# Half sets of exponentials on VectorE in a fused attention and graph-layer kernel

## Chip, cores and metric

The kernel runs on one core of a Trainium2 chip. The metric is the device time in microseconds (us) from the launch's first to its last instruction; runs of the same kernel agree within about 0.03% here. All matrix work is in fp32 or in the fp32r form, nothing is in bf16.

## What is computed

The reference takes 3327 tokens `x` of width 128 and a weighted adjacency matrix `adj` (3327 x 3327), and applies four layers, each followed by a residual and a layer norm. Cut to what matters here:

```python
# layer 0: attention with 128 heads of width 8, adj added twice to the scores
q = (x @ Wq.T).reshape(d, n, h)          # d = 128 heads, h = 8
k = (x @ Wk.T).reshape(d, n, h)
v = (x @ Wv.T).reshape(d, n, h)
a = jnp.einsum('dnh,dmh->dnm', q, k) * d ** -0.5 + adj + adj
a = jax.nn.softmax(a, axis=2)
out = jnp.einsum('dnm,dmh->dnh', a, v).reshape(n, h * d) @ Wo.T
# layer 1: a_norm @ (x @ W.T + b), a_norm from adj + I and its row sums
# layer 2: (adj / rowsum) @ x @ W_in + (adj.T / colsum) @ x @ W_out
# layer 3: x @ W_self.T + (adj @ x) @ W_neigh.T + b
# after every layer: x = layernorm(x + layer)
```

There are 128 x 3327 x 3327 = 1.4 billion exponentials in layer 0. They are the work that the change is about. The column sums of `adj` are used in layer 2 alone.

## The kernel before

**Stages.** A first stage (about 0 to 297 us) projects `x` to queries, keys and values and stores them. `attention()` (297 to 9970 us) is layer 0. A last stage (from 9970 us) divides by the softmax sums, multiplies by `Wo`, and does layers 1 to 3 as dense products with `adj`, 26 row tiles each (`gather`, L1110). A function `wide_attention`, taken when scores could overflow, does not run with these inputs.

**Blocks, heads, sets.** `attention()` goes over 7 query chunks of 476 columns (CW) and, inside each, 4 key blocks of 7, 7, 6 and 6 key tiles of 128 keys (KBS): 28 blocks, called kind 0, 1, 2 and 3 here by their place in the chunk. In a block it goes over 128 heads `d`. The key tiles of a head are taken in three *sets*: 3, 2 and 2 tiles for a block of 7, 2, 2 and 2 for a block of 6 (SETS). Each of the three sets has its own score buffer in PSUM, `sc0`, `sc1`, `sc2`, one bank of 512 columns for each tile. Four heads make a *group* (12 sets, numbered p0 to p11 below), of which there are 32 in a block.

**One set** (`exponents`, L616). TensorE adds two or three score products to the buffer (L632; the buffer holds the edge weights and earlier heads' scores, so that each head takes the previous scores out as it adds its own). Then the exponentials are read out of PSUM into an SBUF tile `e`: by ScalarE in one activation of 952 or 1428 columns (L640), or, for some sets, by VectorE (`vector_exp`, L590): a clamp and scale to an integer that reads PSUM (L596), two bit operations on it in SBUF (L597, L599), and a polynomial of degree five as five `scalar_tensor_tensor` in SBUF (L602), one after the other. Only L596 holds the score buffer. TensorE cannot add the next head's scores to a buffer until it has been read. A set goes whole to VectorE where `on_vector` (L454) says so for the group and it is p2 of its group: 24 of 32 groups in kind 0, all 32 in kind 1, 28 in kinds 2 and 3.

**Weighing** (`weigh`, L647). The sums over keys of a group are taken while the next group's exponentials are made: for each key tile, four products `values x e` for the four heads side by side (L658), into one bank `o`, 8 instructions (each fp32 product goes in two). After which sets of the next group they are placed on TensorE's queue is written in PLACES (blocks of 6: after p0, p2, p4, p6, p8, p10; blocks of 7: p1, p1, p4, p6, p8, p10, p10), FULL (kind 0, a pattern for each of four groups in turn) and FIRST (the first group of a block). Every third group `flush` copies or adds `o` into `acc` on VectorE (L669, L671) before `o` can be used again.

**Order.** TensorE's, ScalarE's, VectorE's and GpSimd's queues run in the order in which the program emits instructions (`manual_schedule`, L685 and after). VectorE's polynomial steps wait in a list `vec` and are emitted by `vector_work` (L607) before each set, as long as a model clock of VectorE (`clock[1]`, a cost in us for each step) is behind a model clock of ScalarE (`clock[0]`, 0.95 or 0.84 a set). VectorE also turns query rows for the next group in kind 0 (`copy_queries`, L517 to L519) and, in the background, transposes `adj` and takes its maxima, row sums and column sums by pieces (`piece_work`, L213: L218, L223, L225, L229 to L233), 91 pieces, one in eight groups.

Of the kernel before, what the change touches and what calls it, by code (L numbers as in the profile page):

```python
# [19 lines left out]
P = 128  # L20
# [10 lines left out]
POLY = (-0.12145248055458069, 1.287218689918518, 0.8447736501693726, 0.7106341123580933, 0.24892811477184296)  # L31
# [19 lines left out]
def kernel(ctx: ExitStack, tc: tile.TileContext, x, adj, wq, wk, wv, wo,  # L51
# [83 lines left out]
    colsum = const.tile([P, T], F32, name="colsum")  # L135
# [20 lines left out]
    csum = const.tile([P, NP // 32], F32, name="csum")  # L156
# [56 lines left out]
    def piece_work(pool, u, c, ai):  # L213

        nj = PIECE // 32
        w = min(PIECE, N - c * PIECE)
        at = pool.tile([P, nj, 4, 32], F32, name="at")
        nc.vector.transpose(at.rearrange("p j t b -> p t j b"), ai.rearrange("p t (j a) -> p t j a", a=32))  # L218
        yield at
        if c == 0:  # L220
            maxima[u] = pool.tile([P, 4, NPC], F32, name="pmax")
            sums[u] = pool.tile([P, 4, NPC], F32, name="psum")
        nc.vector.tensor_reduce(maxima[u][:, :, c], ai[:, :, 0:w], AX.X, ALU.max)  # L223
        yield at
        nc.vector.tensor_reduce(sums[u][:, :, c], ai[:, :, 0:w], AX.X, ALU.add)  # L225
        yield at
        part = csum[:, c * nj:(c + 1) * nj]
        if u == 1:
            nc.vector.tensor_reduce(part, at.rearrange("p j t b -> p j (t b)"), AX.X, ALU.add)  # L229
        else:  # L230
            cs = pool.tile([P, nj], F32, name="cs")
            nc.vector.tensor_reduce(cs, at.rearrange("p j t b -> p j (t b)"), AX.X, ALU.add)
            nc.vector.tensor_tensor(part, part, cs, ALU.add)  # L233
        yield at

    def store_tops(pool, u, top, n):

        hi = pool.tile([P, 4], F32R, name="rhi")
        nc.vector.tensor_copy(hi, top)
        lo = pool.tile([P, 4], F32R, name="rlo")  # L240
        nc.vector.tensor_tensor(lo, top, hi.bitcast(F32), ALU.subtract)
        for row, sb in enumerate((hi, lo)):
            for i in range(P // n):
                nc.gpsimd.dma_start(out=flat_ap(lead_s[u], row * SUPER + i * P, [[1, n], [n, 4]]),
                                    in_=sb[n * i:n * i + n, :].bitcast(F32))
# [172 lines left out]
    def attention():  # L418
        with tc.tile_pool(name="ed", bufs=1) as ed, tc.tile_pool(name="kq", bufs=3) as kq, \
# [11 lines left out]
            o = psc.tile([P, 512], F32, name="o")  # L431
            subs = [(j, min(P, CW - j)) for j in range(0, CW, P)]
# [21 lines left out]
            def on_vector(kb, g):  # L454

                return g % 4 != 0 if kb == 0 else KBS[kb][1] == 7 or g % 8 != 0
# [5 lines left out]
            PLACES = {7: (1, 1, 4, 6, 8, 10, 10), 6: (0, 2, 4, 6, 8, 10)}  # L462
# [79 lines left out]
            loaded, worked, turning = [], [], []  # L542

            def background(n):
                if n % PACE == 2 and worked:
                    piece_store(pe, *worked.pop(0))
# [4 lines left out]
            def background_work(n):  # L551
                if n % PACE == 4 and loaded:
                    u, c, ai = loaded.pop(0)
                    steps = piece_work(pe, u, c, ai)
                    worked.append((u, c, next(steps)))
                    next(steps)
                    clock[1] += 2.4
                    turning.append(steps)
                if n % PACE == 0 and turning:
                    clock[1] += 2.4  # L560
                    for _ in turning.pop():
                        pass

            def prepare(b, d):

                n = b * NHG + d // GROUP
                if d % GROUP == 0:
                    while any(of is None for _, of, _ in vec):
                        vec.pop(0)[2]()
# [12 lines left out]
                if n + 1 < len(groups) and blocks[groups[n + 1][0]][1] == 0 \  # L582
                        and d % GROUP == 1 - on_vector(blocks[b][1], d // GROUP):
# [6 lines left out]
            def vector_exp(e, x, of):  # L590


                y = ex.tile([P, 2, CW], F32, name="ey")
                t = ex.tile([P, 2, CW], F32, name="et")
                yi, ti = y.bitcast(I32), t.bitcast(I32)
                nc.vector.tensor_scalar(yi, x, -58 * math.log(2.0), 2 ** 24 / math.log(2.0), ALU.max, ALU.mult)  # L596
                vec.append((0.7, of, lambda: nc.vector.tensor_scalar(ti, yi, UPPER, EXPONENT, ALU.bitwise_and,  # L597
                                                                 ALU.bitwise_xor)))
                vec.append((0.7, of, lambda: nc.vector.tensor_scalar(yi, yi, LOWER, QUARTER, ALU.bitwise_and,  # L599
                                                                 ALU.bitwise_or)))  # L600
                for i, a in enumerate(POLY):
                    vec.append((1.2, of, lambda i=i, a=a: nc.vector.scalar_tensor_tensor(  # L602
                        e, e if i else y, a, t if i == len(POLY) - 1 else y, ALU.add, ALU.mult)))

            clock = [0.0, 0.0]

            def vector_work(b):  # L607

                while vec and clock[1] < clock[0]:
                    cost, _, step = vec.pop(0)  # L610
                    step()
                    clock[1] += cost
                clock[0] += 0.95 if KBS[blocks[b][1]][1] == 7 else 0.84
                clock[1] = max(clock[1], clock[0] - 1)

            def exponents(b, d, si):  # L616
# [19 lines left out]
                if on_vector(kb, d // GROUP) and (d % GROUP, si) == (0, 2):  # L636
                    vector_exp(e[:, 0:n, :], s[:, 0:n, 0:CW], (b, d // GROUP))
                    clock[1] += 1.2
                else:
                    nc.scalar.activation(e[:, 0:n, :], s[:, 0:n, 0:CW], AF.Exp, scale=2.0)  # L640
# [6 lines left out]
            def weigh(b, g, r):  # L647
# [6 lines left out]
                while any(of == (b, g) for _, of, _ in vec) and r >= SETS[len(queue_of)][2][0]:  # L654
                    vec.pop(0)[2]()
                for j in range(GROUP):
                    c = 32 + (tl * GROUP + j) * 32 - u * A1
                    nc.tensor.matmul(o[32 * j:32 * j + 32, 0:CW], lhsT=values[b, g][:m, c:c + 32],  # L658
# [6 lines left out]
            def flush(b, f):  # L665
                kb = blocks[b][1]
                clock[1] += 0.7
# [7 lines left out]
            def store(b, f):  # L675
                nb = min(PACK, NHG - f * PACK)
                for j in range(GROUP):
                    nc.gpsimd.dma_start(  # L678
# [6 lines left out]
            with tc.manual_schedule(engines={mybir.EngineType.PE, mybir.EngineType.Activation,  # L685
# [8 lines left out]
                for b, d in steps:  # L694
# [3 lines left out]
                    for si in range(len(SETS[KBS[blocks[b][1]][1]])):  # L698
                        vector_work(b)
# [335 lines left out]
    pick = act.tile([P, 32], F32, name="pick")  # L1035
    nc.vector.tensor_tensor(pick, ident[:, 0:32], ident[:, 32:64], ALU.add)
    nc.vector.tensor_tensor(pick, pick, ident[:, 64:96], ALU.add)
    nc.vector.tensor_tensor(pick, pick, ident[:, 96:128], ALU.add)
    ps = bank(7)
    nc.tensor.matmul(ps[0:32, 0:NP // 32], lhsT=pick, rhs=csum, start=True, stop=True)  # L1040
    for q in range(4):
        nc.vector.tensor_copy(colsum[32 * q:32 * q + 32, :],
                              ps[0:32, 0:NP // 32].rearrange("a (s q) -> a q s", q=4)[:, q, :])

# [17 lines left out]
    inv_col = inverse_degree(colsum, "inv_col")  # L1062
# [34 lines left out]

    def gather(t, y, col, b, meanwhile=()):
# [13 lines left out]
        for _, what in todo:  # L1112
            what()
        return ps
# [4 lines left out]
    def divide(t):  # L1119
# [7 lines left out]
        nc.gpsimd.tensor_tensor(ons[t][:n], o[:n, 0:H, :], rec[:n, :].unsqueeze(1).to_broadcast([n, H, D]), ALU.mult)  # L1127
# [38 lines left out]
    with tc.manual_schedule(engines={mybir.EngineType.PE, mybir.EngineType.SP}):  # L1166
# [18 lines left out]
        for t in range(T):  # L1185
# [9 lines left out]
            norm(n, h[:n, :], xs[1][:n, t, :])  # L1195

# [77 lines left out]
```

## Times and profile before

| what | us |
|---|---|
| median of 3 runs (10736.26 to 10739.44) | 10736.91 |
| profiled execution | 10739.45 |
| its span, first to last instruction | 10737.5 |
| granted TensorE clock over the span | 0.996 |
| one block of kind 0, of kind 1, of kind 2 or 3 | about 368, 368, 320 |
| from the last exponential to the end | about 771 |

The blocks' lengths are read off the timeline, from the first edge transposition of a block (L625) to that of the next. The profile's page gives busy time and share of the span for each engine, a picture of the span in 40 slices, the chain that ended last, and the costliest groups of instructions, each with its count, busy time, mean duration, and the idle time of its engine just before it with what ended that idle time. Durations of neighbouring instructions of one engine overlap a little: ScalarE's activations of 952 columns last about 1.0 us each in the profile, but follow each other every 0.844 us in the timeline. [...]

### The profile page before, as it was taken

How to read it: one execution, taken by the hardware profiler on the slowest of the kernel's cores; microseconds unless marked ns; L12 is line 12 of the kernel's file. 1: busy time of each engine (PE TensorE's matmuls, PEld its weight loads, DVE VectorE, ACT ScalarE, POOL GpSimd, SP SyncE). 2: the span in 40 equal slices, each digit the busy share in tenths (PEclk: the TensorE clock that was granted, in tenths of full speed). 3: DMA queues.
4: the chain of work that ended last, by engine and by line, in shares of the span. 5: the costliest groups of instructions: out<-in, count | busy, mean ns of one | idle time of the engine just before them, and what ended most of it. 6: DMA issues, size and time to landing. Idle time of an engine off the chain costs nothing. (4 is left out here: it accounts for less than half of the span.)

```text
span 10737.5 us, 200822 instructions
## 1 busy us (share of the span) xinstructions
PE 10565.1 (98%) x76941; PEld 4105.8 (38%) x76941; DVE 7960.2 (74%) x8554; ACT 9584.8 (89%) x10447; POOL 1554.7 (14%) x2739
## 2 busy tenths in 40 slices
PE   8899999999999999999999999999999999999999
PEld 5333333333333333333333333333333333333779
DVE  6777888777888777887788777888777777777412
ACT  3899999999999999999999999999999999999400
POOL 0111121111221111211122110121111100001200
PEclk9999999999999999999999999999999999999999
DMA  7678886788876888768887588886888867788676
GB/s 270 181 184 188 209 210 181 181 192 201 213 188 171 198 201 209 190 166 200 198 211 196 156 191 191 199 199 172 193 195 202 193 162 179 181 189 196 219 283 246
DMA packets 1013760, 2116.43 MB, mean 197 GB/s; under 512 B 206759, under 2 KB 730985, under 8 KB 998979
## 3 DMA queue, kind: packets, MB, share of 16 engines
q1 hardware_dynamic: 932014, 1985.55, 74.4%
q0 software_dynamic: 79392, 116.16, 3.5%
q8 instruction: 623, 10.21, 0.4%
q14 instruction: 335, 2.74, 0.1%
q10 hardware_dynamic: 1396, 1.77, 0.1%
HBM read 1863.03 MB, written 239.54 MB: 196 GB/s over the span
## 5 line engine op out<-in xcount | busy, mean ns | idle before, releaser
L640 ACT ACTIVATE e<-sc 128x952 f32<-128x952 f32 (+1 forms) x9968 | 9360.0, 1085 | 312.1 <-PE sc L632 284.3
L658 PE MATMUL o<-e,v_pad 128*32 128x476 f32 (+1 forms) x46592 | 5647.1, 573 | 39.4 <-DVE acc L671 18.5
L632 PE MATMUL sc<-qt,kt 64*128 64x476 f32 x23296 | 4491.6, 440 | 52.9 <-ACT e L640 33.5
L632 PEld LDWEIGHTS sc<-qt,kt 64*128 64x128 f32 x23296 | 2184.3, 184 | 4433.6 <-ACT e L640 3740.6
L602 DVE SCALAR_TENSOR_TENSOR e<-e,ey 128x952 f32<-128x952 f32 x2352 | 2707.0, 1151 | 77.4
L596 DVE TENSOR_SCALAR ey<-sc 128x952 int32<-128x952 f32 x784 | 901.1, 1149 | 1411.5 <-PE sc L632 1389.9
L658 PEld LDWEIGHTS o<-e,v_pad 128*32 128x32 f32 (+1 forms) x46592 | 1035.2, 108 | 1907.4 <-issue 1885.1
L533 POOL COPY v_pad<-vs 128x192 f32<-128x192 f32 (+1 forms) x896 | 444.5, 522 | 8018.6 <-DMA vs<-v_img 6214.0
L602 DVE SCALAR_TENSOR_TENSOR e<-ey 128x952 f32<-128x952 f32 x784 | 903.4, 1152 | 27.2
L602 DVE SCALAR_TENSOR_TENSOR e<-e,et 128x952 f32<-128x952 f32 x784 | 901.2, 1149 | 22.3
L253 POOL DMA_DIRECT2D adjT_s<-at x1352 | 760.1, 570 | 132.7 <-DMA adjT_s<-at 92.6
L599 DVE TENSOR_SCALAR ey<-ey 128x952 int32<-128x952 int32 x784 | 519.7, 663 | 27.1
L597 DVE TENSOR_SCALAR et<-ey 128x952 int32<-128x952 int32 x784 | 518.3, 661 | 26.9
L1110 PE MATMUL bank<-y,eT 128*128 128x128 f32 (+1 forms) x4056 | 473.9, 276 | 0.4 <-DVE h L1232 0.4
L1110 PEld LDWEIGHTS bank<-y,eT 128*128 128x128 f32 (+1 forms) x4056 | 465.3, 192 | 5.7 <-DVE h L1232 0.6
L671 DVE TENSOR_TENSOR acc<-o,acc 128x476 f32<-128x476 f32 x231 | 150.3, 651 | 281.5 <-PE o L658 280.9
L517 DVE TENSOR_SCALAR qt<-qt 32x1428 fp32r<-32x1428 f32 x224 | 201.7, 900 | 103.2 <-DMA qt<-q_s 89.2
L519 DVE CAST qt<-qt 64x1904 fp32r<-64x1904 f32 x224 | 260.4, 1163 | 7.6
L1070 ACT ACTIVATE rstd<-mv,eps 128x1 f32<-128x1 f32 x104 | 30.4, 292 | 263.6 <-DVE mv L1068 263.6
L678 POOL DMA_DIRECT2D o_s<-acc x308 | 199.4, 651 | 35.4 <-DVE acc L671 20.8
L1213 PE MATMUL bank<-a,y 128*128 128x512 f32 (+2 forms) x364 | 145.5, 562 | 0.0
L362 ACT ACTIVATE hi<-pp 128x1024 fp32r<-128x1024 f32 x52 | 53.0, 1024 | 87.9 <-PE pp L308 86.3
(148 smaller groups left out, 2274.7 us busy)
## 6 DMA issues: line engine op xcount, KB each, us to landing
qt<-qimg SPq DMA_DIRECT2D x1344, 476.0 KB
kt<-k_s SPq DMA_DIRECT2D x5316, 96.0 KB
kt<-k_s SPq DMA_DIRECT2D x1762, 128.0 KB
eT<-adjT_s SPq DMA_DIRECT2D x78, 1664.0 KB
qimg<-qt SPq DMA_DIRECT2D x224, 476.0 KB
vs<-v_img SPq DMA_DIRECT2D x224, 224.0 KB
adjT_s<-at POOLq DMA_DIRECT2D x1352, 32.0 KB, 4.8
vs<-v_img SPq DMA_DIRECT2D x224, 192.0 KB
```

What stands on the lines that cost most here:

```text
L253: nc.gpsimd.dma_start(out=flat_ap(adjT_s, (t * P + 32 * q) * NP + c * PIECE, [[NP, 32], [P, ns], [1, P]]), in_=at[32 * i:32 * i + 32].rear ...
L517: return [(0.9, None, lambda: nc.vector.tensor_scalar(qt[32:64, 1:], qf[0:32, 0:GROUP - 1], -1.0, None, ALU.mult)), (0.4, None, lambda: nc ...
L519: (1.2, None, lambda: nc.vector.tensor_copy(qt[64:128], qf[0:64]))]
L533: nc.gpsimd.tensor_copy(vp[:, 32:32 + nt * GROUP * 32].rearrange("p (x c) -> p x c", c=32)[:, :, 0:H], vs.rearrange("p (x c) -> p x c", c=H))
L596: nc.vector.tensor_scalar(yi, x, -58 * math.log(2.0), 2 ** 24 / math.log(2.0), ALU.max, ALU.mult)
L597: vec.append((0.7, of, lambda: nc.vector.tensor_scalar(ti, yi, UPPER, EXPONENT, ALU.bitwise_and, ALU.bitwise_xor)))
L599: vec.append((0.7, of, lambda: nc.vector.tensor_scalar(yi, yi, LOWER, QUARTER, ALU.bitwise_and, ALU.bitwise_or)))
L602: vec.append((1.2, of, lambda i=i, a=a: nc.vector.scalar_tensor_tensor(e, e if i else y, a, t if i == len(POLY) - 1 else y, ALU.add, ALU.m ...
L632: nc.tensor.matmul(s[:, i, 0:CW], lhsT=kt[64 * rg:64 * rg + 64, k, pos * P:(pos + 1) * P], rhs=qt[64 * rg:64 * rg + 64, k, :], start=False ...
L640: nc.scalar.activation(e[:, 0:n, :], s[:, 0:n, 0:CW], AF.Exp, scale=2.0)
L658: nc.tensor.matmul(o[32 * j:32 * j + 32, 0:CW], lhsT=values[b, g][:m, c:c + 32], rhs=es[b, g * GROUP + j, r][:m, :], start=(r == 0 and u = ...
L1110: nc.tensor.matmul(ps[:n, 0:D], lhsT=e[:m, s, :n], rhs=y[:m, s, col:col + D], start=(s == 0), stop=(s == T - 1))
```

## The change

- **Half sets.** A set that VectorE takes part in is split: VectorE takes the last key tile of it (476 columns), ScalarE the other one or two. `on_vector` is now asked for each set: in kind 0 every sixth (p2 and p8 of each group, but not p8 of every fourth group), in kind 1 every fifth of the running count, in kinds 2 and 3 every sixth (p2 and p8). That makes 1827 half sets (1827 tiles) where 784 whole sets (1568 tiles) were before.
- **Polynomial.** Degree four in place of five: one step less. A constant phase is taken out of the scores (`PHASE`, in `store_tops` and as an immediate bias of ScalarE's activation); it cancels in the softmax.
- **Order.** `vector_work` now looks ahead to the next instruction of VectorE with a fixed place (`next_fixed`) and emits steps and background work that its model clocks let end before it. The clocks' costs are new. The background work of a piece is emitted in three single instructions.
- **Places.** In blocks of 6 the weighing comes after p1, p3, p5, p7, p9, p11.
- **Two sums banks in blocks of 6.** Every other flush period uses the third bank of `sc0`, which is free there.
- **Column sums.** They leave `piece_work` and are taken in layer 1 from the tiles that `gather` loads, one reduction of 128 x 3328 and one small addition for each of 26 tiles.
- **Seam.** The last stores of `attention()` go over SyncE's and ScalarE's queues instead of GpSimd's; the division of the first row tile goes to VectorE.

```diff
-POLY = (-0.12145248055458069, 1.287218689918518, 0.8447736501693726, 0.7106341123580933, 0.24892811477184296)
+POLY = (-0.039287679561190725, 0.7694055213858888, 0.3602062482980112, 0.1471829588776368)
+PHASE = 0.7927868171488225 * math.log(2.0) / 2
...
+            def sums_bank(b, f):
+                return o if KBS[blocks[b][1]][1] == 7 or f % 2 == 0 else sc[0][:, 2, :]
...
-            def on_vector(kb, g):
-
-                return g % 4 != 0 if kb == 0 else KBS[kb][1] == 7 or g % 8 != 0
+            def on_vector(b, d, si):
+
+                kb = blocks[b][1]
+                p = 3 * d + si
+                if kb == 0:
+                    return p % 6 == 2 and p % 48 != 44
+                return p % 5 == 2 if KBS[kb][1] == 7 else p % 6 == 2
...
-            PLACES = {7: (1, 1, 4, 6, 8, 10, 10), 6: (0, 2, 4, 6, 8, 10)}
+            PLACES = {7: (1, 1, 4, 6, 8, 10, 10), 6: (1, 3, 5, 7, 9, 11)}
...
             def vector_exp(e, x, of):
 
-
-                y = ex.tile([P, 2, CW], F32, name="ey")
-                t = ex.tile([P, 2, CW], F32, name="et")
-                yi, ti = y.bitcast(I32), t.bitcast(I32)
+                while sum(to is not None for _, to, _ in vec) > len(POLY):
+                    take()
+                y = ex.tile([P, CW], F32, name="ey", bufs=2)
+                yi, parts = y.bitcast(I32), {}
                 nc.vector.tensor_scalar(yi, x, -58 * math.log(2.0), 2 ** 24 / math.log(2.0), ALU.max, ALU.mult)
...
+                vec.append((0.37, of, power))
+                vec.append((0.37, of, lambda: nc.vector.tensor_scalar(yi, yi, LOWER, QUARTER, ALU.bitwise_and,
+                                                                     ALU.bitwise_or)))
                 for i, a in enumerate(POLY):
-                    vec.append((1.2, of, lambda i=i, a=a: nc.vector.scalar_tensor_tensor(
-                        e, e if i else y, a, t if i == len(POLY) - 1 else y, ALU.add, ALU.mult)))
+                    vec.append((0.61, of, lambda i=i, a=a: step(i, a)))
...
+            COST = (0.0, 0.455, 0.85, 1.265)
+
+            def next_fixed(b, d, si):
+
+                at, nt = clock[0], KBS[blocks[b][1]][1]
+                for _ in range(12):
+                    if on_vector(b, d, si):
+                        return at + 0.15
+                    if nt == 7 and 3 * (d % GROUP) + si == 11 and (d // GROUP % PACK == PACK - 1 or d == D - 1):
+                        return at + 0.3
+                    at += COST[SETS[nt][si][1]]
...
+            def vector_work(b, d, si):
+
+                until = next_fixed(b, d, si)
+                if spare and clock[1] + sum(cost for cost, _, _ in vec) + 1.2 <= until + 0.2 and clock[1] < clock[0] + 0.9:
+                    spare.pop(0)()
+                    clock[1] += 1.2
+                while vec and clock[1] + vec[0][0] <= min(until, clock[0] + 2.4):
+                    take()
+                clock[1] = max(clock[1], clock[0] - 0.3)
...
-                if on_vector(kb, d // GROUP) and (d % GROUP, si) == (0, 2):
-                    vector_exp(e[:, 0:n, :], s[:, 0:n, 0:CW], (b, d // GROUP))
-                    clock[1] += 1.2
-                else:
-                    nc.scalar.activation(e[:, 0:n, :], s[:, 0:n, 0:CW], AF.Exp, scale=2.0)
+                own = n
+                if on_vector(b, d, si):
+                    own = n - 1
+                    vector_exp(e[:, own, :], s[:, own, 0:CW], (b, d // GROUP, t0 + own))
+                    clock[1] = max(clock[1], clock[0]) + 0.62
+                nc.scalar.activation(e[:, 0:own, :], s[:, 0:own, 0:CW], AF.Exp, bias=-2 * PHASE, scale=2.0)
+                clock[0] += COST[own]
...
-                    nc.gpsimd.dma_start(
+                    (nc.gpsimd if not last else (nc.sync, nc.scalar)[j % 2]).dma_start(
...
+    def add_columns(t):
+        part = colsum if t == 0 else small.tile([P, T], F32, name="part")
+        nc.vector.tensor_reduce(part, eTs.pop(t), AX.X, ALU.add)
+        if t:
+            nc.vector.tensor_tensor(colsum, colsum, part, ALU.add)
...
-        nc.gpsimd.tensor_tensor(ons[t][:n], o[:n, 0:H, :], rec[:n, :].unsqueeze(1).to_broadcast([n, H, D]), ALU.mult)
+        (nc.gpsimd if t else nc.vector).tensor_tensor(ons[t][:n], o[:n, 0:H, :], rec[:n, :].unsqueeze(1).to_broadcast([n, H, D]), ALU.mult)
```

## The prediction, made blind

> **What bounds the kernel now.** I read the page's busy times and costliest groups first, then the idle time of ScalarE by cause, then the timeline around one set that VectorE takes.
>
> ```profile
> PE 10565.1 (98%) x76941; PEld 4105.8 (38%) x76941; DVE 7960.2 (74%) x8554; ACT 9584.8 (89%) x10447; POOL 1554.7 (14%) x2739
> ...
> L640 ACT ACTIVATE e<-sc 128x952 f32<-128x952 f32 (+1 forms) x9968 | 9360.0, 1085 | 312.1 <-PE sc L632 284.3
> ...
> L596 DVE TENSOR_SCALAR ey<-sc 128x952 int32<-128x952 f32 x784 | 901.1, 1149 | 1411.5 <-PE sc L632 1389.9
> ```
>
> The exponentials fill 9360 us of the 9669 us of attention: ScalarE is the bound there, and what idle time it has ends with TensorE's scores. VectorE waits 1390 us for scores at the first step of its exponentials: it has room, and comes to that step early. TensorE's 98% is no bound by itself, since it also waits for score buffers.
>
> ```profile
> 3002.80 0.71 PE L632 MATMUL sc<-qt,kt 64*128 64x476 f32 x4
> ...
> 3003.61 1.15 DVE L596 TENSOR_SCALAR ey<-sc 128x952 int32<-128x952 f32 x1 [1.91 <-PE sc L632]
> ...
> 3004.37 0.81 PE L632 MATMUL sc<-qt,kt 64*128 64x476 f32 x4
> ...
> 3004.95 9.53 ACT L640 ACTIVATE e<-sc 128x952 f32<-128x952 f32 x11 [0.30 <-PE sc L632]
> 3005.11 0.16 PEld L658 LDWEIGHTS o<-e,v_pad 128*32 128x32 f32 x8 [0.22 <-issue]
> 3005.11 1.01 PE L658 MATMUL o<-e,v_pad 128*32 128x476 f32 x8
> ```
>
> This is a block of 6. VectorE takes p2 whole, so ScalarE skips 0.84 us, comes to p3 before TensorE has filled it (fill from 3004.37), and waits. Taking every ScalarE start in the timeline, activations of 952 columns follow each other every 0.844 us, of 1428 every 1.241; one tile more or less is therefore 0.397. Summed, ScalarE's work in a block is 354.3, 347.5 and 300.1 us (kinds 0, 1, 2 and 3) of 367.9, 368.0 and about 320: 13.6, 20.5 and 20 us are lost, 522 us over 28 blocks. In kind 1 and in blocks of 6 nearly all of it is lost at p3, 0.57 us a group. So of each 0.84 us that VectorE takes, ScalarE gains only some 0.27.
>
> [...] L671, 476 columns, takes 651. [...] L597 takes 661 where L596 takes 1149. [...] The new bias is an immediate in the built kernel; L640 has none before, so the trace of before cannot show it; I cost it at 0. [...]
>
> **The change, part by part.** *ScalarE's work.* 56, 77 and 64 half sets a block save 0.397 each, where 24, 32 and 28 whole sets saved 0.843: 22.2 for 20.2, 30.6 for 27.0, 25.4 for 23.6. That is 2.0, 3.6, 1.8 and 1.8 us a chunk of four blocks, 64 us in all, if waits stay.
>
> *A new wait.* In the order of the built instructions each of the 1827 activations of a split set waits for VectorE's semaphore at the read of its own set, though the banks differ. Behind it on ScalarE stand all later sets. So ScalarE starts a split set at the earliest 0.11 (scores to VectorE's start, timeline) + 0.65 (L671's price for 476) + 0.05 = 0.81 us after the scores are done. Whether this costs anything depends on the *lead*: the time from the end of a set's last score matmul to the moment when ScalarE is free for it. The timeline of all sets gives, in kind 1, medians of 0.50, 1.36, 0.05 for p0 to p2, 0.96, 0.47, 0.84, 0.72, 1.35, 0.63, 1.40, 0.09 for p4 to p11 (p3, next to VectorE's set, I take as 0.30). Sets that stand first after weighing have little lead.
>
> *Blocks of 6.* New places make runs (p0 p1) W (p2 p3) W (p4 p5) W, so both split sets are first in their run. From the timeline: second fill 0.32 after the first, weighing 0.31 after that, next run 0.93 later, 1.56 together; scores done 0.48 after a first fill starts; a buffer is refilled 1.03 after a two-tile activation starts. With the fill of p2 at 0, VectorE's read ends at 1.24, ScalarE starts p2 at 1.30, p3 at 1.75, p4 at 2.59; the fill of p7 (second in its run, same buffer as p4) starts at 3.62, its weighing at 3.93, the fill of p8 at 4.86. Six sets take 4.86, against 4.68 for TensorE alone and 4.66 for ScalarE alone. Every second time a group's first fill comes, with its semaphores for new keys (p0's two matmuls stand 0.2 apart there), and I add 0.14. A block is 32 x (4.86 + 5.00) + 4 for its start = 319.5 from above, and 32 x 9.36 + 8 + 4 = 311.5 if VectorE's reading is hidden. Before: 320. I take the middle, 315.7, because the read ends late only by 0.2 and the second sums bank takes away waits for `flush` (18.5 us at L671 over the whole run): -4.3, 14 times, -60.
>
> *Kind 1.* Split sets fall on each place of the group in turn. With the leads above the wait is 0.24 on average, and where the next set has little lead another 0.055: 77 x 0.295 = 22.7 from above; from below 0, but then TensorE bounds the block (11.0 a group by summing its runs, 356). ScalarE's 343.9 + 4 for the start + 4 of other waits gives 356 to 374.4. A ScalarE that waits lets TensorE get ahead, so leads grow; middle, 365: -3, 7 times, -21.
>
> *Kind 0.* p2 has 0.67 of lead (0.1 exposed), p8 0.19 with much scatter: after a double weighing, as in two of the four FULL patterns, 0.7 is exposed. 352.3 + 12.9 of other waits + 3 to 15.6 = 368 to 381. Of those other waits 9 us stand at p1 behind double weighings, and a later ScalarE shortens them: I take 370, +2.3, 7 times, +16.
>
> *VectorE.* Steps that depend on each other follow every 0.69 (0.654 + 0.034; the gap at L602 is 1.184 - 1.150), the bit operations every 0.44: 0.69 + 0.88 + 3 x 0.69 + 0.57 = 4.2 a tile. The model clocks say 3.80, so they put VectorE too early. 77 x 4.2 + 6 (flush) + 11 (pieces) = 340 of 365 in kind 1, 286 of 316 in blocks of 6, and in kind 0, with 32 x 2.4 of query rows, 330 of 370. Full, not over; the order shows a step of the polynomial left behind the next read wherever a piece is worked on. I cost lateness at 0; if that cover is gone see the third rival.
>
> *Column sums and seam.* Leaving `piece_work` frees 91 x 1.4 us of VectorE, which is slack. In layer 1 the reduction (L411's 3.6 us for the same size) and norms, 2 us, fit in a row tile's 6.9 us on TensorE and stand after the norm in the order: 0, at most 26 x 1. At the seam TensorE waits 13.5 us before its first transposition for GpSimd's division, which ended 7 us after its operands; one division on VectorE and stores on other queues give -7 (0 to -10).
>
> Sum: -60 - 21 + 16 - 7 = -72 on the profiled execution's 10739.45 (span 10737.5 + 2), 10667; the median of the runs is 2.5 lower. I say 10665.
>
> **Rivals.** (1) *VectorE's read is hidden and the waits vanish.* For it: 522 us of waits to win from, half steps disturb less than whole ones. Against: the lead at first-in-run sets. Blocks of 6 at 311.5 (-119), kind 1 at 356 (-84), kind 0 at 363 (-35), seam -7: 10492. (2) *ScalarE's wait for VectorE's read takes back all the gain*, slower than before. Price 0.81 less the lead, at 1827 places; it decides as soon as the mean exposed wait is over some 0.3. Then blocks of 6 at 319.5 (-7), kind 1 at 374.4 (+45), kind 0 at 381 (+91), seam 0: 10868. (3) *VectorE's queue becomes the bound*: if steps cost 0.1 more each, a tile costs 4.9 and kind 1 needs 394, blocks of 6 331: 182 + 154 more, 11075. Against: all durations it rests on are in the trace.
>
> **Numbers.** Forecast 0.43 (its own range 10600 to 10740), rival 1 0.24, rival 2 0.27, rival 3 0.06. A measurement can tell about 0.2% (21 us) from no change. Faster: 0.33 + 0.24 = 0.57. Same: 0.08 of the forecast and 0.03 of rival 2, 0.11. Slower: 0.02 + 0.24 + 0.06 = 0.32. The range 10490 to 10870 leaves out about half of rival 1's spread on the low side, a fifth of rival 2 and rival 3, some 0.2.
>
> **What would show it.** Blocks of about 370, 365 and 316 us by the edge transpositions. ScalarE's idle time at the activation split between TensorE's scores and VectorE's `ey`; more than 0.3 us a split set on the latter means rival 2, less than 0.05 rival 1. VectorE's idle before `ey` near 0 in kind 1, with `ey` starting over 0.2 after its scores, means rival 3. L671's price holds if `ey` takes 0.65 and a tile's chain 4.2. Wrong would be a change of the last stage by more than 15 us, or kinds 2 and 3 longer than before.

## The result and the profile after

The changed kernel takes 13078.44 us (median of 4 runs, 13066.51 to 13131.83) against 10738.17 us before (median of 4, 10736.26 to 10740.93): a ratio of 1.2189, 95% interval 1.2155 to 1.2222. It is 22% slower; the prediction said 10665 and a range of 10490 to 10870. The profiled execution has a span of 13075.8 us, 2338 more than before.

The page shows it at once: TensorE, ScalarE and VectorE are busy for 1 to 12% more time than before, and for a smaller share of a longer span. The first line is the busy time of the engines; of the second kind, groups of instructions, each has count, busy time, mean ns of one, then the idle time before it and what ended most of that.

```profile
PE 11333.9 (87%) x76939; PEld 4195.0 (32%) x76939; DVE 8899.9 (68%) x14947; ACT 9712.8 (74%) x11231; POOL 1507.3 (12%) x2734
...
PEclk9998879998899988899888999889998899988899
...
L664 ACT ACTIVATE e<-sc 128x952 f32<-128x952 f32 (+2 forms) x10752 | 9489.9, 979 | 2452.7 <-PE sc L655 1403.4
...
L589 DVE TENSOR_SCALAR ey<-sc 128x476 int32<-128x476 f32 x1827 | 1192.5, 653 | 2942.7 <-PE sc L655 2888.8
L683 PE MATMUL sc<-e,v_pad 128*32 128x476 f32 (+1 forms) x10080 | 1710.3, 759 | 1262.2 <-ACT e L664 1245.0
```

ScalarE's idle time before an exponential went from 312 to 2453 us. VectorE is not the bound: it stands 2943 us before its reads, 2889 of them until scores come. TensorE's clock line, all nines before, dips to 8 in a regular pattern. And the last line is a group that did not exist before: weighing (L683) whose output is not `o` but `sc`. Ahead of it TensorE stands for 1262 us, and what it waits for is ScalarE. The list of waits (in total, times, longest) has it as 827 waits of 1.5 us:

```profile
ACT e L664 <- PE sc L655: 1403.4, 1028, 24.6
...
PE sc L683 <- ACT e L664: 1245.0, 827, 2.4
ACT e L664 <- DVE ey L589: 992.0, 882, 4.0
```

The blocks' lengths place the loss (medians of 7 blocks, from edge transposition to edge transposition):

| | kind 0 | kind 1 | kind 2 | kind 3 | last stage |
|---|---|---|---|---|---|
| before | 368 | 368 | 320 | 320 | 771 |
| after | 388 | 377 | 467 | 471 | 840 |
| summed difference, us | +127 | +61 | +1027 | +1055 | +69 |

The five differences add to 2339. Nine tenths are in blocks of 6. The stretches of two blocks of 6, one of kind 0 and one of kind 1 (length; busy time of each engine; then clock, DMA share, GB/s):

```profile
2800.80:3263.70 462.90, 367.13 (x2338) 108.77 (x2336) 280.22 (x478) 316.13 (x384) 53.55 (x107) 0.86 0.63 142
3263.70:3736.80 473.10, 377.12 (x2333) 110.31 (x2329) 280.16 (x472) 316.68 (x385) 72.25 (x136) 0.84 0.61 141
3736.80:4123.40 386.60, 360.92 (x2713) 129.91 (x2709) 324.67 (x515) 367.01 (x385) 57.12 (x99) 1.00 0.63 166
4123.40:4500.00 376.60, 363.78 (x2716) 130.08 (x2714) 327.14 (x561) 355.39 (x385) 54.35 (x105) 1.00 0.84 187
```

In blocks of 6 no engine is full, and the granted clock is 0.86 and 0.84; in blocks of 7 it is 1.00. Inside one block of 6 there are two regimes. A flush period (three groups) that sums into `o` takes 34 us in the median; one that sums into the third bank of `sc0` takes 55. The timeline where one turns into the other (start, length, instruction, idle time before it and its end):

```profile
3011.39 0.85 PE L655 MATMUL sc<-qt,kt 64*128 64x476 f32 x4
...
3016.35 0.85 PE L655 MATMUL sc<-qt,kt 64*128 64x476 f32 x4
...
3023.66 1.01 PE L683 MATMUL o<-e,v_pad 128*32 128x476 f32 x8
...
3026.74 1.01 PE L683 MATMUL sc<-e,v_pad 128*32 128x476 f32 x8 [1.32 <-ACT e L664]
...
3028.27 0.65 DVE L589 TENSOR_SCALAR ey<-sc 128x476 int32<-128x476 f32 x1 [1.02 <-PE sc L655]
3028.96 1.42 ACT L664 ACTIVATE e<-sc 128x476 f32<-128x476 f32 x2 [1.51 <-DVE ey L589]
...
3030.43 1.22 PE L683 MATMUL sc<-e,v_pad 128*32 128x476 f32 x8 [2.07 <-ACT e L664]
...
3031.58 0.77 PE L655 MATMUL sc<-qt,kt 64*128 64x476 f32 x2
```

While the sums go to `o`, six sets take 4.96 us (3011.39 to 3016.35), and weighing waits for nothing. At 3026.74 the sums go into `sc0`'s third bank, and now weighing stands until ScalarE has finished an activation, 1.32 us here, 2.07 there (827 of the run's 1260 weighings into that bank); the next scores are queued behind it on TensorE, so VectorE and ScalarE then have nothing to read (1.02 and 1.51 us). The weighing does not touch the two banks that ScalarE reads. But the bank is a slice of the tile `sc0`, and the tile's readers and writers are put in order as one (the bank as a tile of its own, below, takes 2025 us off): a write to bank 2 waits for the read of banks 0 and 1, and the next fill of banks 0 and 1 stands behind the write to bank 2, and at the end of the period behind `flush` (70 waits, 59 us over the run).

The last stage is read in the chain that ended last, in order of time, in layer 1:

```profile
12401.89 6.81 DMA eT<-adjT_s
12408.73 3.62 DVE part L1117
12414.92 2.97 PE bank L1135 x14
12419.92 6.64 DMA eT<-adjT_s
12426.58 3.62 DVE part L1117
```

The chain runs through the new reduction (L1117): 18.0 us for two row tiles, and thus 9 a tile (8.5 on average from the first of the 26 reductions to the last), where TensorE alone gave 6.35 before. VectorE's own lines show what stands behind it:

```profile
12408.73 3.62 DVE L1117 TENSOR_REDUCE part<-eT 128x26 f32<-128x3328 f32 x1 [4.70 <-DMA eT<-adjT_s]
12412.26 0.28 DVE L1217 TENSOR_TENSOR z<-bank,y 128x128 f32<-128x128 f32 x1
```

VectorE stands 4.70 us until the tile is loaded, reduces it for 3.62 us, and only then takes `z`, the first step of the residual of the row tile in hand.

### The profile page after: what moved, and what is told of

It is laid out like the page before. It is cut to its first block, busy times and chain, and to the rows that moved or that the text cites. A ratio compares the mean times of both kernels' runs of the same rounds, so it can differ in the third digit from the quotient of the medians.

```text
span 13075.8 us, 208059 instructions
## 1 busy us (share of the span) xinstructions
PE 11333.9 (87%) x76939; PEld 4195.0 (32%) x76939; DVE 8899.9 (68%) x14947; ACT 9712.8 (74%) x11231; POOL 1507.3 (12%) x2734
## 5 line engine op out<-in xcount | busy, mean ns | idle before, releaser
L664 ACT ACTIVATE e<-sc 128x952 f32<-128x952 f32 (+2 forms) x10752 | 9489.9, 979 | 2452.7 <-PE sc L655 1403.4
L683 PE MATMUL o<-e,v_pad 128*32 128x476 f32 (+1 forms) x36512 | 4437.0, 578 | 77.6 <-DVE acc L697 41.2
L589 DVE TENSOR_SCALAR ey<-sc 128x476 int32<-128x476 f32 x1827 | 1192.5, 653 | 2942.7 <-PE sc L655 2888.8
L683 PE MATMUL sc<-e,v_pad 128*32 128x476 f32 (+1 forms) x10080 | 1710.3, 759 | 1262.2 <-ACT e L664 1245.0
L596 DVE SCALAR_TENSOR_TENSOR e<-e,ey 128x476 f32<-128x476 f32 x3654 | 2404.6, 658 | 121.7
L683 PEld LDWEIGHTS o<-e,v_pad 128*32 128x32 f32 (+1 forms) x36512 | 841.6, 109 | 1648.9 <-issue 1585.5
L596 DVE SCALAR_TENSOR_TENSOR e<-ey 128x476 f32<-128x476 f32 x1827 | 1196.5, 655 | 61.8
L596 DVE SCALAR_TENSOR_TENSOR e<-e,et 128x476 f32<-128x476 f32 x1827 | 1197.8, 656 | 54.0
L683 PEld LDWEIGHTS sc<-e,v_pad 128*32 128x32 f32 (+1 forms) x10080 | 226.9, 121 | 1852.1 <-ACT e L664 1321.9
L600 DVE TENSOR_SCALAR ey<-ey 128x476 int32<-128x476 int32 x1827 | 752.3, 412 | 63.1
L593 DVE TENSOR_SCALAR et<-ey 128x476 int32<-128x476 int32 x1827 | 744.3, 407 | 42.6
```

What stands on the lines that cost most here:

```text
L593: nc.vector.tensor_scalar(parts["t"].bitcast(I32), yi, UPPER, EXPONENT, ALU.bitwise_and, ALU.bitwise_xor)
L596: nc.vector.scalar_tensor_tensor(e, e if i else y, a, parts["t"] if i == len(POLY) - 1 else y, ALU.add, ALU.mult)
L600: vec.append((0.37, of, lambda: nc.vector.tensor_scalar(yi, yi, LOWER, QUARTER, ALU.bitwise_and, ALU.bitwise_or)))
L664: nc.scalar.activation(e[:, 0:own, :], s[:, 0:own, 0:CW], AF.Exp, bias=-2 * PHASE, scale=2.0)
L683: nc.tensor.matmul(sums_bank(b, g // PACK)[32 * j:32 * j + 32, 0:CW], lhsT=values[b, g][:m, c:c + 32], rhs=es[b, g * GROUP + j, r][:m, :], ...
```

## Experiments

The kernel before took 10744 to 10748 us on the chips of these runs. Times with an interval are medians of four runs, the others single runs. Lengths of blocks are for kinds 0, 1, 2 and 3, each the median of seven blocks.

**The second sums bank, taken away.** In the changed kernel all sums go to `o`:

```diff
-                return o if KBS[blocks[b][1]][1] == 7 or f % 2 == 0 else sc[0][:, 2, :]
+                return o
```

> The changed kernel with one sums bank `o` everywhere, as before the change; all else as changed. Theory (the second sums bank lies inside the score buffer sc0, waits are kept for whole buffers, so every weighing into it waits for ScalarE's reading of sc0 and the next scores wait for the weighing): blocks of 6 fall from about 468 us to 316 to 323, those of 7 stay at 388 and 377, total about 11000 us. Rival A (the half sets and ScalarE's wait for VectorE's read are what stretches the blocks of 6): blocks of 6 stay over 440, total over 12600. Rival B (TensorE's granted clock, 0.86 in these blocks, falls for a reason of its own and stretches them): the clock stays at 0.86 and the blocks at over 400.

Measured: 11332.13 us, ratio 1.0546 (1.0528 to 1.0564). 1746 of the 2340 us are gone, the clock is back at 0.987, blocks of 7 are unchanged (388, 378). Blocks of 6 come to 343, worse than the 316 to 323 expected: with one bank and the new places, weighing waits for `flush`.

```profile
ACT e L664 <- DVE ey L589: 530.1, 575, 5.0
PE o L683 <- DVE acc L697: 273.2, 196, 2.1
```

The second line (total, times, longest) shows 273 us where TensorE waits for VectorE to empty `o`. So the second bank had a reason, and where it lies is the fault.

**The second sums bank, put alone into the kernel before.** The same function in the old kernel, with nothing else of the change.

> The kernel before with one part of the change alone: in blocks of 6 every other flush period weighs into the third bank of sc0. Theory (whole-buffer waits): blocks of 6 grow from 320 to about 450 to 480, total 12600 to 13000 us, TensorE's weighing waits for ScalarE's activations. Rival A (half sets): at most a few us off 10737, since nothing of the exponentials is changed.

Measured: 12671.08 us, as expected. Blocks of 6 go from 320 to 458, blocks of 7 stay at 368, the clock falls to 0.907. The bank alone costs 1923 us, without half sets, new places or new order:

```profile
ACT e L643 <- PE sc L635: 2112.5, 1843, 23.9
PE sc L661 <- ACT e L643: 1061.4, 835, 2.0
```

**The second sums bank as a tile of its own.** The changed kernel, with `sc0` cut to two banks and the third bank a tile `third`. In blocks of 7 it is still the third bank of a set of three, so ScalarE's activation of three tiles becomes two instructions.

```diff
-            sc = [psc.tile([P, n, 512], F32, name=f"sc{i}") for i, n in enumerate((3, 2, 2))]
+            sc = [psc.tile([P, 2, 512], F32, name=f"sc{i}") for i in range(3)]
+            third = psc.tile([P, 512], F32, name="third")
...
-                return o if KBS[blocks[b][1]][1] == 7 or f % 2 == 0 else sc[0][:, 2, :]
+                return o if KBS[blocks[b][1]][1] == 7 or f % 2 == 0 else third
```

> The changed kernel, with the third score bank of sc0 made a buffer of its own; the second sums bank of the blocks of 6 is the same PSUM bank, now in a buffer that no score of these blocks shares. In blocks of 7 the activation of three tiles becomes one of two and one of one, which costs them about 0.05 to 0.2 us a head. Theory (whole-buffer waits, not the bank): blocks of 6 at 314 to 323, as with one bank, blocks of 7 at 385 to 410. Rival C (the use of two sums banks by turns, or the bank itself, is what hurts): blocks of 6 stay over 440.

Measured: 11053.81 us, clock 0.993, blocks 391, 377, 323, 323. As before, the sums go by turns to `o` and to a bank that no score of these blocks uses, after the same sets; what is different is that this bank is no longer a slice of a score tile, and 2025 us are gone. (Whether it is the same one of the PSUM's banks the traces do not show.) Together with the two runs before, this settles the main cause. It also shows that the waits on the sums are gone and small ones are left:

```profile
ACT e L668 <- DVE ey L590: 213.7, 349, 5.3
ACT e L668 <- PE sc L659: 110.9, 166, 24.5
...
PE o L689 <- DVE acc L703: 34.4, 45, 1.4
```

**The column sums, alone in the kernel before.** They leave `piece_work` and are taken in layer 1, as in the change.

> The kernel before with one part of the change alone: column sums leave the background work and are taken in layer 1. Theory (in VectorE's order the reduction of a tile four ahead stands before a tile's residual, and waits for its load): layer 1 grows from about 6.35 to 9.3 us a row tile, total +50 to +75 us, 10790 to 10812. My prediction's step: +0 to +26. Rival (the last stage grew because its start was disturbed): +0.

Measured: 10822.99 us, ratio 1.0068 (1.0052 to 1.0085), 75 us more, 11 above the range expected, with attention unchanged. The chain shows what the changed kernel's shows:

```profile
10218.81 6.98 DMA eT<-adjT_s
10225.81 3.62 DVE part L1080
10232.00 2.99 PE bank L1098 x14
...
10237.96 6.61 DMA eT<-adjT_s
10244.60 3.62 DVE part L1080
```

In VectorE's order the reduction of a tile loaded four row tiles ahead stands in front of the residual of the present one. The reduction waits for the load, the residual waits behind the reduction, the next load waits for the buffer.

**The places of the weighing.** The version with its own tile, with the places of before in blocks of 6.

```diff
-            PLACES = {7: (1, 1, 4, 6, 8, 10, 10), 6: (1, 3, 5, 7, 9, 11)}
+            PLACES = {7: (1, 1, 4, 6, 8, 10, 10), 6: (0, 2, 4, 6, 8, 10)}
```

> e6 with the old places of weighing in blocks of 6 (after p0, p2, ...), which makes each split set the second of its run, with 0.9 us of lead in the kernel before. My recurrence (six sets in 4.68 where first-in-run gives 4.86): blocks of 6 fall from 323 to 311 to 317, the others stay; total 10890 to 10980 us. Rival (lead is not what decides, VectorE's queue is): 320 or more, total over 11020.

Measured: 10903.14 us; blocks of 6 at 310 and 311 instead of 323, blocks of 7 as before it (390, 377). The new places cost 12 us a block of 6.

**Who reads a split set first.** The version with its own tile, with ScalarE's activation ahead of VectorE's read in the order.

```diff
-                if on_vector(b, d, si):
-                    own = n - 1
-                    vector_exp(e[:, own, :], at_bank(s, own)[:, 0:CW], (b, d // GROUP, t0 + own))
...
+                own = n - 1 if on_vector(b, d, si) else n
...
+                if own < n:
+                    vector_exp(e[:, own, :], at_bank(s, own)[:, 0:CW], (b, d // GROUP, t0 + own))
```

> The run with the third bank as a buffer of its own (e6), with one edit: in a split set ScalarE's activation is emitted ahead of VectorE's read, so that VectorE waits for ScalarE and not ScalarE for VectorE. Theory 1 (what is left over before, some 310 us, is mostly ScalarE's wait for VectorE's read, my second rival): ScalarE's waits for `ey`, 214 us in e6, vanish, kind 0 falls from 388 to 375 to 382, kind 1 from 377 to 367 to 373, blocks of 6 from 323 to 312 to 320, total 10800 to 10950 us. Theory 2 (it is VectorE's whole load and its late reads, whoever goes first): the score buffers come free later still, total 11050 to 11300.

Measured: 11162.68 us, 109 more than with VectorE first (394, 390, 323, 322): the expectation that this order is better fell. The wait has only turned round:

```profile
DVE ey L590 <- ACT e L664: 1164.1, 1387, 9.0
ACT e L664 <- PE sc L659: 425.8, 522, 24.5
```

Both this edit and the old places, in one kernel:

> e7 and e8 together. If both theories hold their gains overlap in blocks of 6 (second in its run, the wait is hidden either way): blocks of 6 at 310 to 317, kinds 0 and 1 as in e7, total 10780 to 10900 us. If ScalarE first only moves the wait, blocks of 6 are slower than in e8.

Measured: 11053.29 us (393, 388, 315, 314), a miss: this order is worse with the old places too.

**Fewer half sets in kind 0.** With its own tile, only p2 is split there (32 half sets in place of 56).

```diff
-                    return p % 6 == 2 and p % 48 != 44
+                    return p % 12 == 2
```

> e6 with kind 0 left at one split set a group, p2; p8 goes to ScalarE whole (24 half sets a block less, 9.5 us more of ScalarE's work). Theory (p8, behind a double weighing, has no lead, so its split costs more than it saves): kind 0 at 380 or less, against 387 to 391 in e6; the rest stays. Rival (the work decides): kind 0 at 395 or more.

Measured: 11007.9 us, kind 0 at 383 in place of 391, 3 over the theory's bound of 380 and far from the rival's 395. The 24 half sets left out had made the block longer, although ScalarE now does 9.1 us more: each had taken 0.381 off it, since its activations follow each other every 0.463 us with 476 columns and every 0.844 with 952. The starts in the changed kernel's timeline agree (how they are read stands under the version that splits only sets of three): behind `ey` ScalarE loses 11.9 us a block of kind 0 at the 24 half sets on p8, 0.50 each, and 6.6 at the 32 on p2, 0.21 each.

**A lighter VectorE.** With own tile and old places, two of the four polynomial steps are left out.

> Leaves out two of the four polynomial steps, so that VectorE's exponentials are wrong and its load a tile falls from 4.2 to 2.8 us. Theory (the blocks of 7 lose because ScalarE stands until VectorE has read the split set's score buffer, whatever else VectorE has to do): only the part of the lateness that comes from a full queue goes, blocks of kind 0 and 1 stay at 382 to 392 and 372 to 378, total 10820 to 10900. Rival (VectorE's load makes its read late): blocks fall to 368 to 374 and 360 to 368, total 10730 to 10800.

Measured: 10857.83 us; kind 0 385.6, kind 1 374.9. That is 4.5 and 1.9 us a block for a third of VectorE's chain: the rival, that VectorE's load makes its read late, falls.

**Half sets without a shared buffer.** With own tile and old places, the same number of half sets, but in blocks of 7 only sets of three tiles are split, so that VectorE reads `third` and ScalarE the two-bank tile.

```diff
-                    return p % 6 == 2 and p % 48 != 44
-                return p % 5 == 2 if KBS[kb][1] == 7 else p % 6 == 2
+                    return p % 6 == 0 and p % 48 != 42
+                return p % 15 in (0, 6, 12) if KBS[kb][1] == 7 else p % 6 == 2
```

> Same number of half sets a block (56 and 77) and same load on VectorE, but in blocks of 7 only sets of three tiles are split, whose third tile has a PSUM tile of its own: ScalarE's activation of the first two and VectorE's read have no buffer in common. Theory (the wait is for the shared buffer): ScalarE's wait for ey nearly vanishes in blocks of 7, kind 0 362 to 374, kind 1 356 to 366, total 10690 to 10790. Rival (VectorE's load, or the mere number of half sets, costs it): 382 to 392 and 372 to 378, total about 10900.

Measured: 10846.18 us, kind 0 384.5, kind 1 375.4: the theory's 362 to 374 and 356 to 366 fell as well, and both blocks lie in the rival's ranges. Its mechanism is real, ScalarE's wait for `ey` over the run is 40.8 us in place of 182.6, but the time did not follow.

What came in its place can be worked out from the starts of ScalarE's activations in the timelines. The next activation starts 0.463, 0.844 or 1.241 us after one of 476, 952 or 1428 columns when nothing holds it; this is its own work (larger with the own tile, where a set of three takes two activations). What a start comes later is put down to the wait that the profile names there. In us a block, medians of seven blocks, from a block's first activation to that of the next (the version without VectorE exponentials is the next experiment):

| kind | version | whole | own work | behind `ey` | behind scores | rest |
|---|---|---|---|---|---|---|
| 0 | before | 368 | 355 | 0 | 6 | 7 |
| 0 | no VectorE exponentials | 387 | 375 | 0 | 5 | 7 |
| 0 | changed kernel | 388 | 354 | 18 | 12 | 4 |
| 0 | own tile, old places | 389 | 362 | 16 | 10 | 1 |
| 0 | the same, only sets of three split | 384 | 357 | 0 | 26 | 1 |
| 1 | before | 368 | 348 | 0 | 19 | 1 |
| 1 | no VectorE exponentials | 382 | 375 | 0 | 1 | 5 |
| 1 | changed kernel | 377 | 345 | 21 | 8 | 2 |
| 1 | own tile, old places | 376 | 352 | 12 | 13 | 0 |
| 1 | the same, only sets of three split | 375 | 348 | 0 | 26 | 2 |

With the shared buffer about half or more of what ScalarE loses is behind VectorE's read. Without it, the version loses as much as the one that it is compared with (26 us in kind 0, 25 in kind 1), but all of it behind TensorE's scores. And a good part of what this version gained is no gain of the buffers: a set of three that is split has no second activation here, so ScalarE has 4.6 and 4.3 us a block less to do, against 5.6 and 1.4 us by which the blocks are shorter. VectorE's read was also not always in time in this version, in kind 0 over 0.6 us after the last scores at a quarter of the half sets, so that it is not a test of the shared buffer alone.

**No VectorE exponentials in blocks of 7.** The version with one sums bank, and `on_vector` false in blocks of 7.

> The change with one sums bank throughout and no VectorE exponentials in blocks of 7 (the blocks of 6 keep theirs). ScalarE then has 128 x (2 x 0.843 + 1.240) = 374.5 us of activations in every block of 7. Theory (half sets in blocks of 7 gain next to nothing, since what ScalarE no longer does comes back as waiting): 377 to 383 in kinds 0 and 1 alike, that is less than the 387 measured with 56 half sets in kind 0 and within 6 of the 377 with 77 in kind 1. Rival (half sets do take work off the path, and something else in these blocks is slow): 395 or more in kind 0 and 388 or more in kind 1.

Measured: 11361.19 us; kind 0 386.5, kind 1 382.3 (with half sets and the same bank 387.5 and 377.9). In kind 0 the theory's point held, though its range ended 3.5 too low: 56 half sets take 21 us of activations off ScalarE and the block is no shorter. In kind 1, 77 take 30 off and 4.4 are kept.

**Versions meant to be faster than both.** Blocks of 7 as before the change (whole sets on p2), blocks of 6 with half sets and the old places, column sums as before, the short polynomial everywhere. First with one sums bank:

> A version meant to be faster than both: blocks of 7 as before the change (whole sets on VectorE, one sums bank) but with the shorter polynomial, blocks of 6 with half sets, the old places of the weighing and one sums bank, column sums where they were before. Blocks of 7 at 362 to 369. Blocks of 6: with one bank and new places 343 was measured; if the places matter as much there as with two banks, 330, which is more than 320: total 10800 to 10900. If half sets win with one bank too (312 to 316), 10620 to 10680.

Measured: 10749.45 us, no gain, and between the two ranges expected (367, 367, 321, 322): with one bank, weighing waits 173.6 us for `flush`. Then with the second bank in its own tile:

> As the other mixed version, but with the second sums bank as a PSUM tile of its own, so that ScalarE's activation of three tiles is two instructions in blocks of 7. Blocks of 6 at 310 to 312 as with that tile and the old places; blocks of 7 368 plus 128 more instructions of some 0.06 us where ScalarE is late, less what the shorter polynomial gives: 366 to 376; last stage 771 to 775. Total 10738 - 14 x 9 + 14 x (-2 to +8) = 10585 to 10725; slower than before only if the divided activation costs over 9 us a block.

Measured: 10622.29 us, ratio 0.9889 (0.9872 to 0.9905), blocks 371, 367, 310, 310. And with a whole set in all 32 groups of kind 0:

> The mixed version with its own tile for the second sums bank, with a whole set on VectorE in all 32 groups of kind 0 in place of 24. ScalarE does 8 x 0.84 = 6.7 less in each of 7 blocks; VectorE's work goes from 275 to some 316 of 371. If the gain stands as it does in kind 1: kind 0 at 366 to 368, total 10590 to 10605. If turning the query rows and the exponentials collide on VectorE: kind 0 at 371 to 378, total 10620 to 10670.

Measured: 10614.7 us, ratio 0.9879 (0.9863 to 0.9896), blocks 371, 367, 310, 311. Kind 0 did not move, so that step brought nothing there (the two intervals overlap); 8 x 0.84 us off ScalarE were again not kept. Of the last version:

```profile
PE 10429.4 (98%) x76941; PEld 4025.7 (38%) x76941; DVE 8288.2 (78%) x11691; ACT 9591.1 (90%) x12575; POOL 1510.7 (14%) x2734
...
L674 ACT ACTIVATE e<-sc 128x952 f32<-128x952 f32 (+1 forms) x10304 | 8905.6, 985 | 176.6 <-PE sc L664 101.7
```

ScalarE's idle time at its exponentials is 177 us, against 312 before.

## Why the prediction was wrong, point by point

- **Blocks of 6, "the second sums bank takes away waits for `flush`", -60: wrong, +2082.** This is the step that failed. It took the bank as a free resource because no set of two uses it, and looked only at what is stored there, not at which buffer it is cut from. The order of the built instructions was read for one new wait, that of ScalarE for VectorE "though the banks differ", and not for the new destination of L683, where the same thing happens. Alone in the old kernel the bank costs 1923 us; as a tile of its own it makes blocks of 6 shorter by 20 (343 to 323), and costs up to 4 us a block of 7 for the divided activation (391 against 388 in kind 0, 371 against 367 in the two mixed versions).
- **The same blocks, the recurrence.** It gave 4.86 to 5.0 us for six sets; with the sums in `o` the trace has 4.96. Where the bank is harmless the blocks take 323 for a predicted 311.5 to 319.5, so this term was still 7 short of its middle: VectorE's reading was taken as half hidden, and by its starts ScalarE loses 22 us a block behind `ey` there. That the new places put both split sets first in their run was priced, but not set against the old places: with those the loss behind `ey` is 3 to 4 us, and 12 us a block come back. And the bank's worth was sized from 18.5 us of waits in a kernel with the old places: with the new places it is 343 less 323, with the old 321 less 310, so 11 to 20 a block.
- **Kinds 1 and 0, -21 and +16: measured +61 and +127.** The direction of the second rival was right (+45 and +91), the measured loss is 1.4 times its size. Two terms failed. The work taken off was put too high: 0.397 a half set is the price of a third tile, and most half sets take the second of two, which is 0.381; with that, the "64 us in all" are 38. And part of the wait for VectorE's read was to go as ScalarE falls behind and TensorE gets ahead ("so leads grow"). It did not: in kind 1 ScalarE loses 21 us behind `ey` where 22.7 was the price from above, and 10 elsewhere where 8 stood (4 of them for the block's start); in kind 0 it loses 18 where 3 to 15.6 was priced, and 16 elsewhere for 12.9. In kind 0 the half sets on p8 lose more there than they save. (Two slips in the recorded sums, 374.4 for 374.6 and 315.7 for 315.5, change nothing.)
- **What is open in the same blocks.** Taking the waits for `ey` away did not give the time back: ScalarE then waited for scores. With a lighter VectorE, or without the shared buffer, the blocks come only 1 to 6 us nearer to before's; with whole sets they are at 367 to 371. That ScalarE and TensorE need nearly the same time there (348 to 355 us a block by ScalarE's starts, and 356 by the prediction's estimate from the runs of TensorE's timeline), so that ScalarE cannot get ahead of TensorE by having less to do, fits the table above, and so do the waits of before: TensorE's weight loads for scores stood 3741 us over the run for ScalarE's reads, and ScalarE 284 us for scores. No run takes that alone, so it is argued, not shown.
- **VectorE's queue, cost 0: right.** `ey` takes 653 ns as priced from L671, starts 0.11 to 0.12 us after its scores in the median of each kind of block, and a third less work on VectorE changed little (4.5 and 1.9 us a block). The steps follow each other every 0.69 us and the bit operations every 0.44, as estimated. The third rival falls.
- **The new bias of ScalarE's activation, cost 0: right.** Activations of 952 columns that wait for nothing follow each other every 0.844 us in the median, before and after.
- **Column sums, "stand after the norm in the order: 0, at most 26": wrong, +75.** The reduction of a later tile stands before the residual of the present one, and the load before it. The fit of 3.6 + 2 us into 6.9 was right as a sum of work, and no help against the order.
- **Seam, -7: right.** From the last exponential to the first transposition of layer 0's output (`on`) TensorE needs 18.2 us where it needed 24.6, -6.5; with +75 this is the last stage's +69.
- **Rivals.** None was a wait that the second bank brings. The sign given for the second, more than 0.3 us behind `ey` a split set, was about met in blocks of 7 (0.33 in kind 0, 0.27 in kind 1). The text named as wrong "a change of the last stage by more than 15 us, or kinds 2 and 3 longer than before"; both came.

## What to carry to other kernels

A spare bank inside a larger tile was not spare here, since waits were kept per tile: it cost 1923 us in the old kernel, and a tile of its own took 2025 us off the new one. Before counting on such a bank, look up in the built order what the first instruction that writes it waits for, and who waits for that write. Work taken off a bounding engine need not come off the time: in kind 0 21 us were taken off and none kept, and a test with that work put back told it. (That such work counts only where the engine that feeds it is ahead is the author's reading, not shown.) And a long reduction that waits for a load belongs behind the short steps on which the next tile hangs: in front of them it cost 75 us here, though its 3.6 us and the norms' 2 had room in a row tile's 6.9.

## What was not expected of the hardware

- TensorE's granted clock was 0.86 and 0.84 over the two blocks of 6 shown above, and 1.00 over the two blocks of 7. Its record in these blocks of 6 holds only 0.5 and 1.0, 0.5 for 27 and 32% of the time. Around the timeline above it is 1.0 until 3031.09, 0.5 until 3034.51, and 0.5 again from 3041.33 to 3054.99, though TensorE is never idle for more than 2.07 us at a time in that block and 2.41 in the next. Over the whole run it is 0.918; without the waits at L683 it is 0.987 (one bank) and 0.993 (own tile), and 0.907 with the bank put alone into the kernel before. So the low clock comes and goes with those waits; by what it is set the runs do not show. A weighing of eight took 1.22 us instead of 1.01 where the clock fell. How much of the loss is the clock and how much the wait was not separated.
- Reads of PSUM by ScalarE and VectorE at the same time, from different tiles, hardly slowed each other. In the changed kernel 157 activations of 952 columns, each followed by the next without a wait, overlap an `ey` read of another score buffer by over 0.4 us; the next starts 0.844 us after them in the median, as after the 4893 that overlap none, and the reads take 0.654 in the median. Before, where `ey` reads 952 columns, it is 0.862 (179 activations) against 0.844 (7188). In the version that splits only sets of three, in three blocks of 7, it is 0.843 against 0.844, and the reads take 0.654. What ScalarE waited for in the change was the read of its own set's buffer: 992 us over the run, and 40.8 in place of 182.6 where blocks of 7 no longer shared it.
- The sums had a bank of their own throughout. That was not enough: TensorE stood 1245 us for ScalarE before it weighed into the slice of `sc0`. With a tile of its own no such wait is among the run's 60 longest, which go down to 17 us.
